# One-hot graph attention: row maxima and a gather in place of scores, softmax and two products

## The chip, the cores and the metric

The kernel runs on one core of a Trainium2 chip. A core has TensorE (PE: matrix products and transposes), VectorE (DVE), ScalarE (ACT), GpSimd (POOL) and SyncE (SP, which here only issues DMAs), and 16 DMA engines that all queues share. The metric is the device time of one execution in microseconds (us). The profile's span runs from the first to the last instruction of one profiled execution.

## The reference

Inputs: x (4096 x 512), adj (4096 x 4096), W (512 x 2048, four heads of 512 columns), a (4 x 1024 x 1); all f32, and so is the output (4096 x 512).

```python
ht  = (x @ W).reshape(N, 4, 512).transpose(1, 0, 2)        # one slice per head
src = einsum('hnd,hd->hn', ht, a[:, :512, 0])
dst = einsum('hnd,hd->hn', ht, a[:, 512:, 0])
e   = leaky_relu(src[:, :, None] + dst[:, None, :], 0.01) + adj[None]
att = softmax(e, axis=-1)
h   = einsum('hij,hjd->hid', att, ht).mean(axis=0)
out = layernorm(x + h, axis=-1)                            # eps 1e-5, no weights
```

How adj is made matters here: a random graph with a full diagonal, whose present edges have a weight drawn evenly from 0.05 to 1e9, and 0 where there is no edge.

```python
_a = jax.random.uniform(..., (4096, 4096)) < _pij
_a = jnp.logical_or(_a, jnp.eye(4096, dtype=bool))
adj = _a.astype(jnp.float32) * jax.random.uniform(..., (4096, 4096), jnp.float32, 0.05, 1e+09)
```

## The kernel before

P = 128, C = 512; NB = 32 blocks of rows, KB = 4 blocks of features, NCH = 8 chunks of columns, H = 4 heads. x, W and the row of dst for each head, copied to all partitions, stay on chip. A unit is one block of 128 rows of one head, 128 units in all. Per unit and chunk of 512 columns:

```python
nc.scalar.activation(s, dst_b[:, h, ts(c, C)], AF.Identity, bias=src[:, ib, h : h + 1])   # L153
nc.vector.scalar_tensor_tensor(s, s, SLOPE, s, op0=OP.mult, op1=OP.max)                   # L154
nc.vector.tensor_tensor_reduce(out=s, in0=s, in1=adj_t[ib, k][:, ts(part, C)], scale=1.0,
    scalar=LOWEST, op0=OP.add, op1=OP.max, accum_out=self.m[:, c : c + 1])                # L156
# ... largest of the eight (L164), then
nc.scalar.activation(s, s, AF.Exp, bias=self.nm, accum_out=self.z[:, c : c + 1])          # L168
for q in range(Q):
    nc.tensor.transpose(ps[:, q, :], self.s[c][:, ts(q, P)], ident)                       # L173
# ... copied from PSUM by ACT (L176) or DVE (L178), then
for q in range(Q):
    nc.tensor.matmul(self.y_ps, pt[:, q, :], x_sb[:, c * Q + q, :], ...)                  # L186
```

Then per unit the divisor (L193 to L197), four transposes of y (L202), a copy (L204), and the projection:

```python
for kb in range(KB):
    nc.tensor.matmul(o_ps[ib], self.yt[:, kb, :], w_sb[:, kb, ts(h, D)], ...)             # L211
```

and per block of rows, after its four heads, the residual and the norm:

```python
nc.vector.tensor_add(r, o_ps.pop(ib), x_sb[:, ib, :])                                     # L217
nc.vector.bn_stats(st, r)                                                                 # L219
nc.vector.bn_aggr(mv, st)                                                                 # L221
nc.vector.tensor_scalar_add(sd, mv[:, 1:2], EPS)                                          # L223
nc.scalar.activation(sd, sd, AF.Sqrt)                                                     # L224
# ... one unit later
nc.vector.reciprocal(sd, sd)                                                              # L230
nc.vector.tensor_scalar(r, r, mv[:, 0:1], sd, op0=OP.subtract, op1=OP.mult)               # L231
nc.gpsimd.dma_start(out[ts(self.ib, P), :], r)                                            # L232
```

Of the kernel before, what the change touches and what calls it, by code (L numbers as in the profile page):

```python
# [9 lines left out]
F32 = mybir.dt.float32  # L10
AF = mybir.ActivationFunctionType
# [3 lines left out]
SLOPE = 0.01  # L15
EPS = 1e-5
LOWEST = -3.4028234663852886e38


@with_exitstack  # L20
def gat_resnorm_kernel(
# [8 lines left out]
    """layernorm(x + mean_h softmax(leaky_relu(src_i + dst_j) + adj) @ (x @ W_h)).  # L30

    The attention rows are applied to x first and the result to W_h after it:
    x stays on chip for the whole launch, x @ W would not fit. Likewise
    src = x @ (W_h a_src) and dst = x @ (W_h a_dst).
    A unit of work is a block of 128 rows of one head. Its scores are made in
    chunks of 512 columns while the unit before it is in the matrix products.
    """
    nc = tc.nc
    P = 128
    N, D = x.shape  # L40
    H = a.shape[0]
    KB = D // P          # blocks of features
    NB = N // P          # blocks of rows
    C = 512              # columns of a chunk
    NCH = N // C
    Q = C // P           # blocks of rows in a chunk
    AW = 2               # chunks in a tile of adj

    ctx.enter_context(tc.manual_schedule())

    const = ctx.enter_context(tc.tile_pool(name="const", bufs=1))
    x_sb = const.tile([P, NB, D], F32, name="x_sb")
    w_sb = const.tile([P, KB, H * D], F32, name="w_sb")
    dst_b = const.tile([P, H, N], F32, name="dst_b")
    src = const.tile([P, NB, H], F32, name="src")
    ident = const.tile([P, P], F32, name="ident")

# [4 lines left out]
    with ExitStack() as pre:  # L62
        once = pre.enter_context(tc.tile_pool(name="once", bufs=1))
        two = pre.enter_context(tc.tile_pool(name="two", bufs=2))
        pps = pre.enter_context(tc.tile_pool(name="pps", bufs=2, space=bass.MemoryType.PSUM))

        a_b = once.tile([P, H, 2 * D], F32, name="a_b")
        nc.scalar.dma_start(
            a_b.rearrange("p h m -> p (h m)"),
            bass.AP(tensor=a.tensor, offset=a.offset, ap=[[0, P], [1, H * 2 * D]]),  # L70
        )
        for kb in range(KB):
            nc.scalar.dma_start(w_sb[:, kb, :], w_blocks[:, kb, :])
        for g in range(NCH):
            nc.sync.dma_start(x_sb[:, ts(g, Q), :], x_blocks[:, ts(g, Q), :])
        make_identity(nc, ident)

        v = once.tile([P, KB, 2 * H], F32, name="v")
        prod = once.tile([P, D], F32, name="prod")
        for kb in range(KB):  # L80
            for s in range(2):
                for h in range(H):
                    nc.vector.scalar_tensor_tensor(  # L83
                        prod, w_sb[:, kb, ts(h, D)], 1.0, a_b[:, h, ts(s, D)],
                        op0=OP.mult, op1=OP.mult,
                        accum_out=v[:, kb, s * H + h : s * H + h + 1],
                    )

        def x_transposed(g):
            xT = two.tile([P, KB, C], F32, name="xT")  # L90
            for q in range(Q):
                ps = pps.tile([P, KB, P], F32, name="ps_x")
                for kb in range(KB):
                    nc.tensor.transpose(ps[:, kb, :], x_sb[:, g * Q + q, ts(kb, P)], ident)  # L94
                nc.scalar.copy(xT[:, :, ts(q, P)], ps)  # L95
            return xT

        def scores(g, xT):
# [3 lines left out]
            sd = two.tile([2 * H, C], F32, name="sd")  # L102
            nc.vector.tensor_copy(sd, ps)  # L103
            for h in range(H):
                pb = pps.tile([P, C], F32, name="ps_b")
                one_hot = ident[: 2 * H, H + h : H + h + 1].to_broadcast([2 * H, P])
                nc.tensor.matmul(pb, one_hot, sd, start=True, stop=True)  # L107
                nc.vector.tensor_copy(dst_b[:, h, ts(g, C)], pb)
            pt = pps.tile([P, Q, 2 * H], F32, name="ps_s")
            for q in range(Q):  # L110
                nc.tensor.transpose(pt[:, q, :], sd[:, ts(q, P)], ident[: 2 * H, : 2 * H])  # L111
            nc.vector.tensor_copy(src[:, ts(g, Q), :], pt[:, :, :H])

        xT = x_transposed(0)
        for g in range(NCH):
            ahead = x_transposed(g + 1) if g + 1 < NCH else None
            scores(g, xT)
            xT = ahead

# [1 line left out]
    adj_pool = ctx.enter_context(tc.tile_pool(name="adj_pool", bufs=1))  # L121
    s_pool = ctx.enter_context(tc.tile_pool(name="s_pool", bufs=9))
    pt_pool = ctx.enter_context(tc.tile_pool(name="pt_pool", bufs=3))
    y_pool = ctx.enter_context(tc.tile_pool(name="y_pool", bufs=2))
    yt_pool = ctx.enter_context(tc.tile_pool(name="yt_pool", bufs=1))
    stat = ctx.enter_context(tc.tile_pool(name="stat", bufs=2))
    psum = ctx.enter_context(tc.tile_pool(name="psum", bufs=2, space=bass.MemoryType.PSUM))

    units = [(ib, h) for ib in range(NB) for h in range(H)]
    adj_t, o_ps, norm = {}, {}, {}  # L130

    def load_adj(ib, k):
        t = adj_pool.tile([P, AW * C], F32, name=f"adj{k}")
        nc.sync.dma_start(t, adj[ts(ib, P), ts(k, AW * C)])
        adj_t[ib, k] = t

    class Unit:
        def __init__(self, n):
            self.ib, self.h = units[n]
            self.s = []  # L140
            self.m = stat.tile([P, NCH], F32, name="m")
            self.z = stat.tile([P, NCH], F32, name="z")
            self.nm = stat.tile([P, 1], F32, name="nm")
            self.rz = stat.tile([P, 1], F32, name="rz")
            self.pt = {}
            self.y_ps = None

        def add(self, c):
            """leaky_relu(src + dst) + adj, and its largest in each row."""
            ib, h = self.ib, self.h  # L150
            s = s_pool.tile([P, C], F32, name="s")
            self.s.append(s)
            nc.scalar.activation(s, dst_b[:, h, ts(c, C)], AF.Identity, bias=src[:, ib, h : h + 1])  # L153
            nc.vector.scalar_tensor_tensor(s, s, SLOPE, s, op0=OP.mult, op1=OP.max)  # L154
            k, part = divmod(c, AW)
            nc.vector.tensor_tensor_reduce(  # L156
                out=s, in0=s, in1=adj_t[ib, k][:, ts(part, C)], scale=1.0, scalar=LOWEST,
                op0=OP.add, op1=OP.max, accum_out=self.m[:, c : c + 1],
            )
            if h == H - 1 and part == AW - 1 and ib + 1 < NB:  # L160
                load_adj(ib + 1, k)

        def largest(self):
            nc.vector.tensor_reduce(self.nm, self.m, axis=AX.X, op=OP.max, negate=True)  # L164

        def exp(self, c):
            s = self.s[c]
            nc.scalar.activation(s, s, AF.Exp, bias=self.nm, accum_out=self.z[:, c : c + 1])  # L168

        def transpose(self, c):  # L170
            ps = psum.tile([P, Q, P], F32, name="pt_ps", bufs=3)
            for q in range(Q):
                nc.tensor.transpose(ps[:, q, :], self.s[c][:, ts(q, P)], ident)  # L173
            pt = pt_pool.tile([P, Q, P], F32, name="pt")
            if c in (1, 3, 5):
                nc.scalar.copy(pt, ps)  # L176
            else:
                nc.vector.tensor_copy(pt, ps)  # L178
            self.pt[c] = pt

        def apply(self, c):
            if c == 0:
                self.y_ps = psum.tile([P, D], F32, name="y_ps")
            pt = self.pt.pop(c)
            for q in range(Q):
                nc.tensor.matmul(  # L186
                    self.y_ps, pt[:, q, :], x_sb[:, c * Q + q, :],
                    start=(c == 0 and q == 0), stop=(c == NCH - 1 and q == Q - 1),
                )

        def scale(self):
            """The softmax's divisor, with that of the mean over heads."""
            nc.vector.tensor_reduce(self.rz, self.z, axis=AX.X, op=OP.add)  # L193
            nc.vector.tensor_scalar_mul(self.rz, self.rz, float(H))
            nc.vector.reciprocal(self.rz, self.rz)
            self.y = y_pool.tile([P, D], F32, name="y")
            nc.vector.tensor_scalar_mul(self.y, self.y_ps, self.rz)  # L197

        def turn(self):
            ps = psum.tile([P, KB, P], F32, name="yt_ps", bufs=1)  # L200
            for kb in range(KB):
                nc.tensor.transpose(ps[:, kb, :], self.y[:, ts(kb, P)], ident)  # L202
            self.yt = yt_pool.tile([P, KB, P], F32, name="yt")
            nc.scalar.copy(self.yt, ps)  # L204

        def project(self):
# [94 lines left out]
```

## Time and profile before

Median of three runs: 4705.16 us (4705.05 to 4705.61). The profiled execution has a span of 4702.5 us.

| What | Value |
|---|---|
| PE busy | 4596.1 us, 14112 instructions |
| DVE busy | 2124.3 us, 4656 instructions |
| ACT busy | 1811.9 us, 3712 instructions |
| POOL busy | 18.2 us |
| HBM read, written | 81.79 MB, 8.39 MB |

How to read the lines that follow further down: a row of the groups gives the line of the kernel, the engine, the operation, output<-input, shapes and count; after the bar the busy time in us and the mean of one in ns; after the second bar the engine's idle time just before these instructions, and what ended it. A row of the windows gives from:to in us and its length, then busy us (and count) of PE, PEld (the weight load), DVE, ACT and POOL, then the granted TensorE clock, the busy share of the 16 DMA engines and the GB/s moved. The granted clock in the whole execution is 0.992 of full.

### The profile page before, as it was taken

The numbers are of one execution on the slowest core, as the hardware profiler recorded it, in microseconds if no ns is written. First come the engines' busy times: TensorE is split into PE (matmuls) and PEld (weight loads), VectorE is DVE, ScalarE is ACT, GpSimd is POOL, SyncE is SP. The second block draws the span as 40 slices with busy tenths as digits, with TensorE's granted clock in tenths as the row PEclk, the third lists the DMA queues.
The fourth block names the chain that finished last, engine by engine and source line by source line (L and its number), as shares of the span: only waits on it lengthen the run. The fifth ranks groups of instructions, "written<-read, shape, count | busy, mean of one in ns | idle before, by whom it ended". The sixth has DMA issues, their size and how long they took to land.

```text
span 4702.5 us, 38848 instructions
## 1 busy us (share of the span) xinstructions
PE 4596.1 (98%) x14112; PEld 2251.0 (48%) x14112; DVE 2124.3 (45%) x4656; ACT 1811.9 (39%) x3712; POOL 18.2 (0%) x38
## 2 busy tenths in 40 slices
PE   7899999999999999999999999999999999999999
PEld 3344444444444444444444444444444444444444
DVE  3444444444444444444444444444444444444443
ACT  1334334334334434433433433433433443343342
POOL 0000000000000000000000000000000000000000
PEclk7999999999999999999999999999999999999999
DMA  3000000000000000000000000000000000000000
GB/s 125 27 12 21 18 21 20 12 12 21 18 21 20 7 16 21 18 21 16 7 21 21 18 21 16 7 21 21 18 21 12 12 21 21 18 21 12 12 21 3
DMA packets 26127, 92.66 MB, mean 20 GB/s; under 512 B 2768, under 2 KB 2768, under 8 KB 25296
## 3 DMA queue, kind: packets, MB, share of 16 engines
q1 hardware_dynamic: 22656, 75.51, 4.7%
q0 software_dynamic: 2560, 8.39, 0.5%
q10 hardware_dynamic: 720, 6.29, 0.3%
q8 instruction: 111, 1.82, 0.2%
q14 instruction: 80, 0.66, 0.0%
HBM read 81.79 MB, written 8.39 MB: 19 GB/s over the span
## 4 chain that ended last, share of the span: by engine, by line
issue 75%; PE 23%; DVE 1%; POOL 0%; DMA 0%; ACT 0%; POOLq 0%; ACTq 0%; DVEq 0%
PE y_ps L186 16%; PE o_ps L211 2%; PE pt_ps L173 2%; PE ps_b L107 1%; PE ps_sd L101 1%; PE ps_x L94 0%; DVE y L197 0%; DVE prod L83 0%; PE yt_ps L202 0%; POOL out_dram L232 0%; DMA w_sb<-in_L_gnn_W_dram 0%; DVE s L154 0%; DVE sd L103 0%; DVE s L156 0%; PE ps_s L111 0%
## 5 line engine op out<-in xcount | busy, mean ns | idle before, releaser
L186 PE MATMUL y_ps<-x_sb,pt 128*128 128x512 f32 x8192 | 3685.7, 593 | 0.0
L186 PEld LDWEIGHTS y_ps<-x_sb,pt 128*128 128x128 f32 x8192 | 1487.1, 190 | 1531.3 <-issue 1530.9
L154 DVE SCALAR_TENSOR_TENSOR s<-s 128x512 f32<-128x512 f32 x1024 | 705.6, 689 | 1048.4 <-ACT s L153 1006.2
L153 ACT ACTIVATE s<-dst_b,src 128x512 f32<-128x512 f32 x1024 | 723.0, 718 | 971.2 <-PE pt_ps L173 952.2
L178 DVE COPY pt<-pt_ps 128x512 f32<-128x512 f32 x640 | 442.6, 692 | 997.4 <-PE pt_ps L173 997.4
L168 ACT ACTIVATE s<-s,nm 128x512 f32<-128x512 f32 x1024 | 724.0, 708 | 181.0 <-DVE nm L164 181.0
L173 PEld LDWEIGHTS pt_ps<-ident,s 128*128 128x128 f32 x4096 | 512.5, 141 | 551.7 <-issue 538.7
L176 ACT COPY pt<-pt_ps 128x512 f32<-128x512 f32 x384 | 225.1, 586 | 1346.4 <-PE pt_ps L173 1346.4
L156 DVE CUSTOM_DVE_ANT_0 s<-s,adj 128x512 f32<-128x512 f32 x1024 | 708.6, 692 | 35.1
L173 PE MATMUL pt_ps<-ident,s 128*128 128x128 f32 x4096 | 615.3, 273 | 12.7 <-ACT s L168 12.7
L211 PE MATMUL o_ps<-w_sb,yt 128*128 128x512 f32 x1024 | 460.8, 593 | 0.7 <-ACT yt L204 0.7
L211 PEld LDWEIGHTS o_ps<-w_sb,yt 128*128 128x128 f32 x1024 | 184.6, 190 | 184.6 <-issue 183.6
L197 DVE TENSOR_SCALAR y<-y_ps,rz 128x512 f32<-128x512 f32 x128 | 96.0, 750 | 296.8 <-PE y_ps L186 296.8
L168 ACT ACTIVATION_READ_ACCUMULATOR s<-s,nm 128x1 f32 x1024 | 191.2, 187 | 0.0
L202 PE MATMUL yt_ps<-ident,y 128*128 128x128 f32 x512 | 83.9, 286 | 52.6 <-DVE y L197 52.6
L204 ACT COPY yt<-yt_ps 128x512 f32<-128x512 f32 x128 | 75.0, 586 | 76.0 <-PE yt_ps L202 76.0
L202 PEld LDWEIGHTS yt_ps<-ident,y 128*128 128x128 f32 x512 | 53.6, 140 | 83.5 <-DVE y L197 83.5
L224 ACT ACTIVATE sd<-sd 128x1 f32<-128x1 f32 x32 | 6.5, 203 | 210.8 <-DVE sd L223 210.8
L156 DVE DVE_READ_ACCUMULATOR2_ANT m<- 128x1 f32 x1024 | 83.8, 82 | 0.0
L217 DVE TENSOR_TENSOR y<-o_ps,x_sb 128x512 f32<-128x512 f32 x32 | 22.1, 692 | 90.2 <-PE o_ps L211 90.2
L94 PE MATMUL ps_x<-ident,x_sb 128*128 128x128 f32 x128 | 29.9, 422 | 21.8 <-DMA x_sb<-in_x_dram 16.6
L95 ACT COPY xT<-ps_x 128x512 f32<-128x512 f32 x32 | 18.7, 586 | 76.8 <-PE ps_x L94 76.8
(31 smaller groups left out, 412.8 us busy)
## 6 DMA issues: line engine op xcount, KB each, us to landing
adj<-in_adj_dram SPq DMA_DIRECT2D x128, 512.0 KB, 3.4
x_sb<-in_x_dram SPq DMA_DIRECT2D x8, 1024.0 KB, 17.9
out_dram<-y POOLq DMA_DIRECT2D x32, 256.0 KB, 2.3
w_sb<-in_L_gnn_W_dram ACTq DMA_DIRECT2D x4, 1024.0 KB, 10.7
a_b<-in_L_gnn_a_dram ACTq DMA_DIRECT2D x1, 2048.0 KB, 8.8
```

What stands on the lines that cost most here:

```text
L153: nc.scalar.activation(s, dst_b[:, h, ts(c, C)], AF.Identity, bias=src[:, ib, h : h + 1])
L154: nc.vector.scalar_tensor_tensor(s, s, SLOPE, s, op0=OP.mult, op1=OP.max)
L156: nc.vector.tensor_tensor_reduce(out=s, in0=s, in1=adj_t[ib, k][:, ts(part, C)], scale=1.0, scalar=LOWEST, op0=OP.add, op1=OP.max, accum_o ...
L168: nc.scalar.activation(s, s, AF.Exp, bias=self.nm, accum_out=self.z[:, c : c + 1])
L173: nc.tensor.transpose(ps[:, q, :], self.s[c][:, ts(q, P)], ident)
L176: nc.scalar.copy(pt, ps)
L178: nc.vector.tensor_copy(pt, ps)
L186: nc.tensor.matmul(self.y_ps, pt[:, q, :], x_sb[:, c * Q + q, :], start=(c == 0 and q == 0), stop=(c == NCH - 1 and q == Q - 1),)
L197: nc.vector.tensor_scalar_mul(self.y, self.y_ps, self.rz)
L202: nc.tensor.transpose(ps[:, kb, :], self.y[:, ts(kb, P)], ident)
L204: nc.scalar.copy(self.yt, ps)
L211: nc.tensor.matmul(o_ps[ib], self.yt[:, kb, :], w_sb[:, kb, ts(h, D)], start=(h == 0 and kb == 0), stop=(h == H - 1 and kb == KB - 1),)
```

## The change

Where the largest adj of a row leads the second largest by more than all that the scores can differ by, plus 110 for the exponential, the softmax row is a one at that column and zeros elsewhere, whatever the scores. Then the block's output is layernorm(x_i + x_j @ mean over heads of W_h), with j the column of the row's maximum. The new kernel computes this for every row, tests the leads meanwhile, and has the general computation as a branch that is entered if any row fails.

A block is now the 128 rows p * 32 + ib, so that a partition's rows of x and of the output lie together in memory. adj is loaded a whole block at a time (128 rows of 16 KB, six slots). The column of a row's maximum is found in two steps: the maxima of 64 segments of 64 columns, the first segment that holds the maximum, a gather of that segment from memory, and the column within it; then the row of x is gathered. Cuts are marked with "...":

```diff
+    leading_rows(tc, x, adj, W, a, out, ident, v, n_bad, any_bad)
+    flag = nc.values_load(any_bad[0:1, 0:1], min_val=0, max_val=N)
+    with tc.If(flag > 0, preferred_fallthrough_block=True, label="general"):
+        general(tc, x, adj, W, out, ident, v, n_bad)
...
+    AHEAD = 5        # adj blocks loaded ahead
+    Q = 4
+    PIECES = 4       # adj pieces of the first and the last four blocks
+    LATE = NB - Q    # 28
+    BEHIND = LATE - Q    # 24
+    adj_pool = ...tile_pool(name="adj_pool", bufs=AHEAD + 1)
...
+    def segment_maxima(ib, lo, hi):
+        ...
+            nc.vector.tensor_reduce(
+                seg_of[ib][:, ts(k, S // n)],
+                adj_t[ib][:, ts(k, N // n)].rearrange("p (s e) -> p s e", e=E), axis=AX.X, op=OP.max)
+    def find_segment(ib):
+        nc.vector.max(out=top[:, ib, :], in_=seg)
+        nc.vector.max_index(at, top[:, ib, :], seg)
+        nc.gpsimd.tensor_tensor(row, at[:, 0:1], first[:, ib : ib + 1], op=OP.add)
+        nc.gpsimd.indirect_dma_start(out=lead, out_offset=None, in_=adj_segs, in_offset=...row...)
+        nc.gpsimd.tensor_tensor(start, at[:, 0:1], width, op=OP.mult)
+    def gather_rows(ib, col):
+        nc.gpsimd.indirect_dma_start(out=y, out_offset=None, in_=x, in_offset=...col...)
+    def find_column(ib):
+        if ib < BEHIND:
+            find_inner(ib)      # nc.vector.max(out=inner[:, ib, :], in_=lead_of[ib])
+        nc.vector.max_index(within, top[:, ib, :], lead_of[ib])
+        nc.gpsimd.tensor_tensor(col, at_of.pop(ib), within[:, 0:1], op=OP.add)
+        gather_rows(ib, col)
+    def find_column_in_row(ib):     # the last block: straight from the row of adj
+        nc.vector.max_index(col, top[:, ib, :], adj_t[ib])
+        gather_rows(ib, col)
...
+    def test():
+        nc.vector.tensor_tensor(gap, top[:, :, 1], inner[:, :, 1], op=OP.max)
+        ...                         # gap = is_gt(0.9999 * (a1 - gap) - 2^-22 * |a1| - lead_by, 0)
...
+    COLUMN, PROJECT, STATS, FINISH = 2, 3, 4, 6
+    for t in range(NB):
+        if t == NB // 2:
+            tc.mark_branch_hint_location("general", engines=HINTED)   # PE, ACT, DVE, POOL
+        if t in x_at:
+            load_x(*x_at[t])
+        load_adj(t + AHEAD)
+        middle = 1 if t > LATE else 2
+        segment_maxima(t, 0, middle)
+        if t >= COLUMN:
+            find_column(t - COLUMN)
+        segment_maxima(t, middle, PIECES)
+        ...
+        find_segment(t)
+        ...                         # t < 15: mean of the heads of W, and W_h a by transposes
+        ib = t - PROJECT
+        if ib >= 0:
+            turn(ib)                # four transposes, copied by ACT
+            if ib < BEHIND:
+                residual(ib)        # x added by a product with the identity
+        ...
+        if ib >= 0:
+            products(ib)            # four products with the mean of the heads
+        if t >= BEHIND + STATS:
+            put_by(t - STATS)
+        elif t >= STATS:
+            stats(t - STATS)        # mean and variance, two ACT passes
+            row_norm(t - STATS)     # a third, for the bound
+        if pair:
+            finish(t - FINISH)
+            finish(t - FINISH + 1)
+    for ib in range(BEHIND, NB, 2):
+        load_x(ib, 2)
+    for ib in range(0, BEHIND, 2):
+        store(nc.sync, ib, 2)
+    find_column(NB - 2)
+    find_column_in_row(NB - 1)
+    ...                             # the last eight blocks, the bound and the test between them
+    finish_last(NB - 4, True)       # add, bn_stats, bn_aggr, sqrt, reciprocal, scale: DVE and ACT
+    ...
+    report(pg)                      # number of failing rows, per block and in all
+    ...
+    finish_in_halves(NB - 1)
+    store(nc.sync, NB - 1, 1)
```

The stores of all 32 blocks are issued after the last load. W lies in the slots of x's blocks 16 to 31 until it has been used. "The branch announced in mid-loop" is the hint in the loop's iteration 16[...]. The general path keeps the computation of before in a plainer order, in a loop over the blocks that enters only blocks with failing rows.

## The prediction

> **What bounds the kernel now.** I read first the busy shares, then the costliest groups, then the chain of waits, and last the DMA rate in narrow windows, because the new kernel will live there.
>
> The busy shares and the first rows of the groups:
>
> ```profile
> PE 4596.1 (98%) x14112; PEld 2251.0 (48%) x14112; DVE 2124.3 (45%) x4656; ACT 1811.9 (39%) x3712; POOL 18.2 (0%) x38
> ...
> L186 PE MATMUL y_ps<-x_sb,pt 128*128 128x512 f32 x8192 | 3685.7, 593 | 0.0
> ```
>
> TensorE is busy all the time, and 8192 of its 14112 instructions are one line: the attention weights times x, 32 products of 128x128 by 128x512 for each of 128 units (32 row blocks by 4 heads). The page warns that PE's busy time isn't PE at its peak; the spacing in the timeline confirms the bound. There the weight loads of L186 start 0.43 us apart (4675.51, 4675.94, 4676.37), and 8192 x 0.43 = 3523 us. Add 1024 products of L211 (440 us) and 4608 transposes at about 0.11 us (four of L173 in 0.60 us, so some 500 us): 4463 us of a span of 4702.5. Idle before L186 is 0.0: no wait sets the end.
>
> The chain of waits and the DMA line say the same from the other side:
>
> ```profile
> issue 75%; PE 23%; DVE 1%; POOL 0%; DMA 0%; ACT 0%; POOLq 0%; ACTq 0%; DVEq 0%
> ...
> DMA packets 26127, 92.66 MB, mean 20 GB/s; under 512 B 2768, under 2 KB 2768, under 8 KB 25296
> ```
>
> Memory carries 20 GB/s over the span. What it can carry shows in the first 40 us, when x, W and a are loaded:
>
> ```profile
> 2.00:3.00 1.00, 0.00 (x0) 0.00 (x0) 0.00 (x0) 0.00 (x0) 0.00 (x0) 1.00 0.85 317
> ...
> 10.00:12.00 2.00, 0.00 (x0) 0.00 (x0) 0.00 (x0) 0.00 (x0) 0.00 (x0) 1.00 1.01 419
> 12.00:14.00 2.00, 0.00 (x0) 0.00 (x0) 1.01 (x3) 0.00 (x0) 0.00 (x0) 1.00 1.03 420
> 14.00:16.00 2.00, 0.00 (x0) 0.00 (x0) 1.90 (x7) 0.00 (x0) 0.00 (x0) 1.00 1.01 413
> 16.00:18.00 2.00, 1.36 (x7) 1.39 (x8) 1.93 (x6) 0.00 (x0) 0.00 (x0) 1.00 1.03 415
> ...
> 30.00:32.00 2.00, 1.61 (x4) 0.10 (x2) 1.93 (x6) 0.00 (x0) 0.00 (x0) 1.00 1.05 387
> 32.00:34.00 2.00, 0.00 (x0) 0.00 (x0) 1.90 (x5) 0.00 (x0) 0.00 (x0) 1.00 1.05 385
> ```
>
> The last two columns are the share of the 16 DMA engines and GB/s. The share is full, so these are ceilings: about 417 GB/s while the 8 KB rows of W run beside x, 385 GB/s when x's 2 KB packets run alone. The first bytes move 2 us after the start.
>
> **What the Trainium skill says.** "DMA: Bandwidth & Descriptors", section Bandwidth, measures 425 GB/s for 16 MB on one core and less for smaller transfers; the 413 to 420 above agree to 2%. "VectorE: DVE Perf Modes", section The perf-mode tier table, gives tensor_reduce one element per cycle only, at 0.96 GHz. No long reduce is in this trace, but other 512-element f32 operations that run at that rate take 689 to 692 ns, which is 533 ns of elements and about 158 ns fixed, and the small tensor_reduce of L164 takes 161 ns: it fits. "TensorE: Matmul & The Clock Gate", Part 1, says that a TensorE with pauses runs at half clock; the windows from 38 to 50 us show a granted clock of 0.50, so I allow for it. "Runtime: NRT & Kernel Launch", section Instruction fetch mechanics, says that a branch taken to instructions that are not fetched yet stalls its engine. No run here shows it so far; the announcement in mid-loop aims at that.
>
> **The change, part by part.**
>
> Removed: all 128 units. adj goes up to 1e9, so a softmax row is nearly always a one at its largest adj and zeros elsewhere. The output row is then layernorm(x_i + x_j(i) @ mean_h W_h). The scores disappear if the test of leads holds. I worked the test out from the inputs as the setup makes them: the bound on all that the scores and the exponential can add is 178.6, and the smallest margin of the 4096 rows after subtracting it is 10474. No row fails, so the general path is skipped and its whole body costs a load of one number and a branch.
>
> Kept: adj must be read once, 67.11 MB. With x (8.39), W (4.19), the gathered x rows (32 x 128 rows of 2 KB, 8.39), the gathered adj segments (31 x 128 pieces of 256 B, 1.02) and the output (8.39), 97.5 MB. Their time when the DMA engines never rest:
>
> - adj, 16 KB rows, at 415 GB/s: 161.7 us.
> - W and x, 8 KB rows, 12.58 MB at 415: 30.3 us.
> - gathered x rows, 2 KB, at 385: 21.8 us.
> - output, mostly 4 KB rows, at 400 (between the two; estimate): 21.0 us.
> - segments: 3968 packets. By bytes 2.6 us; if a 256 B packet cost as much as a 2 KB one (2048 B x 16 / 385 GB/s = 85 ns), 21 us. I take 8 us, an estimate.
>
> Sum 242.8 us.
>
> VectorE per row block: two tensor_reduce of 2048 elements, each 2133 + 150 = 2.28 us (4.57); Max and MaxIndex over 64 elements twice, with the load of the values to be matched, about 6 instructions of some 0.17 us (small DVE groups are 0.15 to 0.18 us): about 5.6 us. DMA per block in the steady part: 2.10 MB of adj (5.05 us), 0.26 of x (0.63), 0.26 gathered (0.68), segments 0.25: 6.6 us. So VectorE waits for data, about 1 us a block. Slots for adj are six, so loads are five blocks ahead, 10 MB or 25 us of traffic, and a late VectorE does not leave the queue empty.
>
> ScalarE per block: yt copy 0.59, two statistics and one row norm at 0.70 + 0.19 each (2.67), the finish 0.70, early a W copy 0.59: 4.5 us. TensorE in all: 169 products of 512 columns at 0.43 = 73 us and about 200 transposes at 0.11 = 22 us, or 190 us at half clock. Both are under 6.6 us a block.
>
> The tail: when the last piece of adj lands, 2.1 MB of x and all 8.4 MB of output are still to move, 26 us that are in the sum. VectorE meanwhile has a serial list: last reduce and segment (1.7), a MaxIndex over all 4096 columns (4.4), three finish_last at about 2.6 (7.8, from the rows of before's end: 0.69 + 0.69 + 0.18 + 0.2 + 0.16 + 0.55), four adds (2.8), inner maxima and test (2.5), report (0.5), the finish in halves (2.3): 22 us and some waits, about 24. So the stores and VectorE end together, and the last block's store then needs its own landing, 2.3 us in before. I add 3 us for that and for gaps in the tail.
>
> Total: 2.0 (first bytes) + 242.8 + 3 (tail) + 2 (the last number read, branch and end) = 249.8 us of span; the time of before is 2.7 us above its span (4705.2 against 4702.5): 252.5. The adj rows are longer than any in the trace and may run at 425 rather than 415, 4 us less. I settle on 250 us, about 19 times faster.
>
> **Rivals.**
>
> 1. VectorE becomes the bound. For: its 5.6 us per block is only 15% under DMA's 6.6. A tensor_reduce that pays something for each of its 32 segments would pass it. At 7 us a block it is 32 x 7 = 224 plus 7 for the first load plus 24 for the tail, 255 plus the end: about 260 us. Against: nothing in this trace costs more than its elements plus 0.16 us.
> 2. The gathers hold up the chain. Each block needs segment, then column, then x row, each gathered by GpSimd behind the bulk loads in the same DMA engines. One costs GpSimd 0.55 us in the plain form (L232); an indexed one surely more. For: DVE executes in order and stands still at find_column if the segment is late. Against: it is used two blocks (13 us) later. If it happens: 5 to 20 us more, 255 to 270.
> 3. The general path runs, or the branch is dear. One failing row would add the general set-up (before's is some 100 us) and some 140 us per failing block (4600/128 = 36 us a unit, four heads). The margin of 10474 speaks against it. A late fetch at the end is a few us at most, beside the last store.
> 4. DMA does better: 425 GB/s on everything and cheap segments: 97.5/0.425 = 229 + 10 = 239 us.
>
> **Range and chances.** Rivals 1 and 2 reach 260 to 268, rival 4 reaches 239. So 238 to 268 eight times in ten. Every one of them is far under 4611 us (2% faster); only the general path on nearly all blocks would not be, and the margins exclude it: faster 0.98, same 0.01, slower 0.01.
>
> **What would show it.** Right: a DMA share near full in nearly all 40 slices with about 400 GB/s; adj the largest landing; DVE 75 to 85% busy with DMA adj as releaser of its reduces; TensorE under half; no rows of the general path. tensor_reduce at about 2.28 us; MaxIndex over 4096 columns at about 4.4 us. Rival 1 would show DVE near 100% and SP waiting for DVE; rival 2 DVE idle released by the gathered segment, and holes in the DMA slices. A wrong prediction most likely comes from the rate on 16 KB rows that lie 512 KB apart (each partition's row is 32 rows from the next), which no trace here has shown, or from the tail's serial list.

## The result and the profile after

The changed kernel takes 244.22 us (median of five runs, 243.78 to 245.87) against 4705.07 before: a ratio of 0.052, 95% interval 0.0518 to 0.0521, or 19 times faster. The prediction was 250 with a range of 238 to 268. The profiled execution has a span of 242.6 us. Its chain of waits is empty on the page, so the bound is read from the DMA line, the waits and the tail's timeline.

From the page after: busy time of each engine, the DMA share and rate in 40 slices of 6 us each, the queues (packets, MB, share of the 16 DMA engines' span; q1 is SyncE's, q0 GpSimd's), and the sum:

```profile
PE 197.3 (81%) x679; PEld 102.2 (42%) x679; DVE 189.1 (78%) x312; ACT 112.4 (46%) x270; POOL 96.4 (40%) x209
...
DMA  6999999999999999999999999999999999999954
GB/s 242 434 407 423 420 428 418 419 436 413 425 416 423 410 425 428 422 415 419 431 417 420 419 430 421 413 421 415 429 427 394 407 406 407 407 415 417 415 202 176
...
q1 hardware_dynamic: 11376, 88.09, 87.7%
q0 software_dynamic: 3584, 9.44, 9.9%
...
HBM read 89.15 MB, written 8.39 MB: 402 GB/s over the span
```

Before, memory moved 20 GB/s and TensorE was busy for 98% of the span. Now the DMA engines are full from the second slice to the 38th, and no other engine is above 81%. The rate is about 420 GB/s up to the 30th slice, about 406 in slices 31 to 35, and falls away in the last two. The rows of the general path are absent: no row failed the test.

The groups of VectorE, shapes apart (count | busy us, mean ns | idle before, releaser):

```profile
L158 DVE TENSOR_REDUCE seg<-adj_t 128x32 f32<-128x2048 f32 x54 | 122.8, 2276 | 32.8 <-DMA adj_t<-in_adj_dram 32.7
...
L201 DVE FIND_INDEX8 col<-top,adj_t 128x8 uint32<-128x4096 f32 x1 | 4.4, 4420 | 0.0
```

VectorE's only long idle time is in front of the reduces, and what ends it is adj's arrival. In the timeline two neighbouring blocks that waited for nothing start 5.37 us apart (start, duration):

```profile
126.39 2.27 DVE L158 TENSOR_REDUCE seg<-adj_t 128x32 f32<-128x2048 f32 x1
...
131.76 2.27 DVE L158 TENSOR_REDUCE seg<-adj_t 128x32 f32<-128x2048 f32 x1
```

So a block takes VectorE 5.37 us, against 6.3 us that memory needs for it (2.65 MB at 420 GB/s).

The waits, of the whole kernel (us in total, times, longest):

```profile
DVE seg L158 <- DMA adj_t<-in_adj_dram: 38.4, 23, 5.6
...
PE tp L208 <- DMA y<-in_x_dram,col: 11.8, 9, 3.7
...
DVE within L193 <- DMA lead<-in_adj_dram,row: 1.8, 2, 1.6
```

The gathered segment held VectorE up for 1.8 us in all.

The end, in windows (from:to, length, busy us of PE, PEld, DVE, ACT, POOL, clock, DMA share, GB/s):

```profile
226.00:228.00 2.00, 2.00 (x7) 0.97 (x6) 1.79 (x13) 1.97 (x6) 0.43 (x2) 1.00 1.02 416
228.00:230.00 2.00, 2.00 (x11) 0.92 (x10) 1.36 (x3) 1.60 (x6) 0.73 (x2) 1.00 1.03 420
230.00:232.00 2.00, 2.00 (x11) 1.77 (x11) 1.04 (x5) 2.00 (x4) 0.00 (x0) 1.00 0.75 298
232.00:234.00 2.00, 1.58 (x8) 1.04 (x6) 0.81 (x4) 1.03 (x4) 0.00 (x0) 1.00 0.92 355
234.00:236.00 2.00, 0.00 (x0) 0.00 (x0) 1.53 (x5) 0.72 (x2) 0.00 (x0) 1.00 0.13 45
236.00:238.00 2.00, 0.00 (x0) 0.00 (x0) 1.57 (x6) 1.28 (x3) 0.00 (x0) 1.00 0.42 158
238.00:240.00 2.00, 0.00 (x0) 0.00 (x0) 0.82 (x2) 0.00 (x0) 0.00 (x0) 0.68 0.75 297
240.00:241.00 1.00, 0.00 (x0) 0.00 (x0) 0.00 (x0) 0.00 (x0) 0.00 (x0) 0.50 0.43 156
```

Up to 230 us the stores keep memory full; after that it waits for the last blocks. From 230 to the end 2.5 MB move, which at 420 GB/s is 5.9 of 12.6 us: 6.7 us of memory time are lost here, and some 2.5 in the first 4 us. The rest of the span, 233.4 us, is traffic, at 419 GB/s on average.

### The profile page after: what moved, and what is told of

The parts are those of the page before. It is cut to its first block, busy times and chain, and to the rows that moved or that the text cites. A ratio compares the mean times of both kernels' runs of the same rounds, so it can differ in the third digit from the quotient of the medians.

```text
span 242.6 us, 2510 instructions
## 1 busy us (share of the span) xinstructions
PE 197.3 (81%) x679; PEld 102.2 (42%) x679; DVE 189.1 (78%) x312; ACT 112.4 (46%) x270; POOL 96.4 (40%) x209
## 3 DMA queue, kind: packets, MB, share of 16 engines
q0 software_dynamic: 3584, 9.44, 9.9%
## 4 chain that ended last, share of the span: by engine, by line
## 5 line engine op out<-in xcount | busy, mean ns | idle before, releaser
L158 DVE TENSOR_REDUCE seg<-adj_t 128x32 f32<-128x2048 f32 (+1 forms) x74 | 146.3, 1987 | 38.6 <-DMA adj_t<-in_adj_dram 38.4
L221 PE MATMUL o<-w_sum,yt 128*128 128x512 f32 x248 | 117.1, 614 | 4.2 <-ACT yt L210 4.2
L221 PEld LDWEIGHTS o<-w_sum,yt 128*128 128x128 f32 x248 | 45.9, 195 | 58.9 <-issue 47.5
L210 ACT COPY yt<-tp 128x512 f32<-128x512 f32 x32 | 18.8, 587 | 50.4 <-PE tp L208 45.8
L181 POOL DMA_INDIRECT y<-in_x_dram,col x32 | 30.8, 963 | 18.6 <-POOL col L195 15.2
L171 POOL DMA_INDIRECT lead<-in_adj_dram,row x32 | 32.2, 1008 | 14.2 <-POOL row L169 14.2
L311 PE MATMUL o<-hold,ident 128*128 128x512 f32 x32 | 18.9, 745 | 16.4 <-DMA hold<-in_L_gnn_W_dram 16.4
L208 PE MATMUL tp<-ident,y 128*128 128x128 f32 x128 | 20.1, 281 | 11.9 <-DMA y<-in_x_dram,col 11.8
L214 PE MATMUL o<-hold,ident 128*128 128x512 f32 x48 | 26.3, 631 | 0.6 <-DMA hold<-in_x_dram 0.6
L228 ACT ACTIVATE sq<-hold 128x512 f32<-128x512 f32 x32 | 19.8, 620 | 0.0
L311 PEld LDWEIGHTS o<-hold,ident 128*128 128x128 f32 x32 | 7.3, 239 | 25.7 <-POOL row L169 12.0
L261 ACT ACTIVATE hold<-o,nm,sd 128x512 f32<-128x512 f32 x24 | 17.2, 771 | 0.0
```

The costliest lines, as they stand in the source:

```text
L158: nc.vector.tensor_reduce(seg_of[ib][:, ts(k, S // n)], adj_t[ib][:, ts(k, N // n)].rearrange("p (s e) -> p s e", e=E), axis=AX.X, op=OP.max,)
L171: nc.gpsimd.indirect_dma_start(out=lead, out_offset=None, in_=adj_segs, in_offset=bass.IndirectOffsetOnAxis(ap=row[:, :1], axis=0),)
L181: nc.gpsimd.indirect_dma_start(out=y, out_offset=None, in_=x, in_offset=bass.IndirectOffsetOnAxis(ap=col[:, :1], axis=0),)
L208: nc.tensor.transpose(tp[:, kb, :], y[:, ts(kb, P)], ident)
L210: nc.scalar.copy(yt, tp)
L214: nc.tensor.matmul(o_ps[ib], ident, hold[:, ib, :], start=True, stop=False)
```

## The experiments

Theory: the time is now the traffic, 97.7 MB, plus a short head and a tail. Rivals: VectorE (78% busy) sets it; the chain of gathers sets it; the test and the branch cost a part. A difference of less than 0.6 us can't be read: the changed kernel itself gave 244.22 and, on the chip of the two branch runs and the first late test, 244.85 (243.58 to 245.85). The runs come from several chips; the kernel before took 4705.1 to 4706.2 us on each of them.

> The changed kernel again, on the same chip as the next three, so that differences of a microsecond can be read. Every theory: 244 us, between 243.5 and 246.

### Half of the traffic

Only half of adj's columns are loaded, and VectorE goes over them twice; there is no branch. The output is that of half an adj.

```diff
-                nc.sync.dma_start(t[:, ts(k, N // n)], adj_rows[ib][:, ts(k, N // n)])
+                nc.sync.dma_start(t[:, ts(k, w)], adj_rows[ib][:, ts(k, w)])   # first half only
...
-                adj_t[ib][:, ts(k, N // n)]...
+                adj_t[ib][:, ts(k % (n // 2), N // n)]...                      # read twice
```

> From the variant without branch: only the first 2048 columns of adj are loaded (33.6 MB less), and VectorE reduces them twice, so that its work per block stays 5.36 us; the last block's search over a whole row is over 2048 columns (2.2 us less). The output is not the reference's. Memory theory (the 97.7 MB at about 420 GB/s set the time): VectorE now becomes the bound, 7 us for the first piece + 32 x 5.36 + 27 for the tail, 200 to 212 us. VectorE theory (its 78% busy time sets the end): 240 to 243, only the 2.2 us less. Gather theory (the chain of segment, column and row sets the pace): 230 to 243.

Measured: 220.55 us (219.83 to 222.46), 23.5 us less than without branch (below). The traffic, 64.1 MB, would allow 80 us less. So bytes do set the time, and the next bound lies close behind; but it is not VectorE alone, for which 200 to 212 us were expected. The windows of this run:

```profile
20.00:40.00 20.00, 19.70 (x94) 12.50 (x94) 18.89 (x29) 5.50 (x12) 8.73 (x18) 1.00 1.02 415
40.00:60.00 20.00, 20.00 (x84) 11.65 (x83) 16.31 (x28) 11.28 (x30) 8.70 (x20) 1.00 1.01 414
...
80.00:100.00 20.00, 20.00 (x92) 12.20 (x90) 15.50 (x25) 12.20 (x31) 9.95 (x22) 1.00 0.67 243
100.00:120.00 20.00, 20.00 (x62) 9.49 (x62) 15.49 (x27) 14.28 (x34) 9.06 (x19) 1.00 0.61 227
120.00:140.00 20.00, 19.65 (x58) 8.85 (x57) 19.49 (x31) 13.22 (x35) 11.09 (x25) 1.00 0.79 290
140.00:160.00 20.00, 18.71 (x55) 8.09 (x54) 19.45 (x29) 11.91 (x29) 11.98 (x25) 1.00 0.74 241
```

The first busy figure is TensorE: 20.00 of 20.00 from 40 to 120 us, while memory falls to 227 GB/s and VectorE to 15.5. In this stretch TensorE also works on W and a (the products with a end at 100 us), and VectorE waits 11.2 us in all for two late segments and for results of the bound. From 120 to 160 us it is VectorE that hardly pauses: 19.5 of 20, at 5.36 us a block. So the next bound is first TensorE and then VectorE. The same stretches of the changed kernel itself:

```profile
40.00:60.00 20.00, 19.36 (x93) 12.33 (x94) 15.96 (x24) 7.50 (x19) 7.06 (x14) 1.00 1.01 421
60.00:80.00 20.00, 19.66 (x85) 11.49 (x83) 15.99 (x25) 12.15 (x29) 9.17 (x21) 1.00 1.02 423
...
140.00:160.00 20.00, 15.41 (x44) 6.57 (x43) 17.28 (x25) 10.53 (x27) 9.58 (x19) 1.00 1.00 417
```

While W and a are worked on, TensorE, VectorE and memory lie within a fifth of each other; memory is the one that is full throughout.

### Half of VectorE's work

adj is loaded in full, but only its first half is reduced; no branch; the output is again that of half an adj.

```diff
         for k in range(lo * n // PIECES, hi * n // PIECES):
+            if k >= n // 2:
+                continue
```

> From the variant without branch: adj is loaded in full, but VectorE reduces only the first half of its columns (2.28 us less per block, 73 us in all). The output is not the reference's. Memory theory: the last piece of adj lands as before, VectorE is 2 to 3 us earlier in the tail: 239 to 243. VectorE theory: 170 to 190.

Measured: 241.89 us (241.43 to 242.02), 2.1 us less than without branch. Its busy line and its longest wait:

```profile
PE 196.9 (82%) x679; PEld 102.8 (43%) x679; DVE 114.7 (48%) x275; ACT 112.1 (47%) x270; POOL 96.6 (40%) x209
...
DVE seg L157 <- DMA adj_t<-in_adj_dram: 105.3, 31, 9.4
```

VectorE lost 74 us of work, and 67 of them came back as waiting for adj (105.3 us against 38.4). That VectorE's work in all sets the time is excluded; 74 us less of it are worth 2.1 us.

### One block of lag for the gather

```diff
-    COLUMN, PROJECT, STATS, FINISH = 2, 3, 4, 6
+    COLUMN, PROJECT, STATS, FINISH = 1, 3, 4, 6
...
-    find_column(NB - 2)      # now in the loop
```

> The column within the segment is looked for one block after the segment is found, not two. A gathered segment lands a median 6.0 us after its issue, and some 1.5 us pass before that; with one block of lag VectorE has 2.3 us of other work in between. Gather theory: VectorE waits some 4 to 5 us in every block, 32 x 10 + 29 = 330 to 360 us. Memory theory with slack (the queue stays five blocks ahead and absorbs most of it): under 260.

Measured: 362.87 us (360.68 to 364.89), 118.6 more, slightly over the expected range. The waits of this run:

```profile
DVE inner L187 <- DMA lead<-in_adj_dram,row: 114.3, 23, 6.5
...
DVE within L193 <- DMA lead<-in_adj_dram,row: 28.6, 7, 6.6
...
DVE seg L158 <- DMA adj_t<-in_adj_dram: 12.8, 5, 5.6
```

The two waits for segments, 142.9 us in 30 blocks, less the 25.6 us that VectorE no longer waits for adj, come to 117.3: nearly the whole loss. A gathered segment needs about 7 us from its search to its landing (about 6 of them from the issue), and one block later is too early by 4 to 5 us in nearly every block; VectorE stands still until it is there. The lag of two is what makes the gathers free; the rival was real and the code had bought it off.

### The stores in the loop

```diff
         load_adj(t + AHEAD)
+        if FINISH + 2 <= t < BEHIND + FINISH + 2 and t % 2 == 0:
+            store(nc.sync, t - FINISH - 2, 2)
...
-    for ib in range(0, BEHIND, 2):
-        store(nc.sync, ib, 2)
```

> The stores of blocks 0 to 23 are issued in the loop, two blocks after they are finished, not after the last load. The bytes are the same. Memory theory: the last piece of adj lands about 15 us later (6.3 MB at 420 GB/s), and VectorE's tail of 29 us then has only 4.2 MB of traffic beside it: 253 to 258. Rival (reads and writes side by side run faster than reads alone): 244 or less.

Measured: 257.91 us (257.33 to 258.65), 13 us more with the same bytes. The windows of this run:

```profile
160.00:200.00 40.00, 32.32 (x81) 14.85 (x82) 31.23 (x44) 18.34 (x47) 18.36 (x39) 0.87 1.01 419
...
226.00:256.00 30.00, 16.30 (x55) 9.00 (x53) 17.23 (x50) 16.68 (x45) 2.86 (x5) 0.78 0.34 129
```

Memory is as full as before up to 226 us, and then runs at 129 GB/s for 30 us, because little is left to move while VectorE, TensorE and ScalarE work off the last blocks. The last reduce ends at 222.8 us and not at 213.1, 9.7 us later where 15 were expected, and the tail after it takes 33.4 us where it took 29.5. Holding the stores back is worth 13 us.

### The tail in another order

The last block's column is taken from its gathered segment, as in the other blocks, in place of the 4.4 us search; adds, statistics and block 30's norm come earlier.

```diff
     find_column(NB - 2)
-    find_column_in_row(NB - 1)
...
+    for ib in range(BEHIND, LATE):
+        add_x(ib)
...
     finish_last(NB - 4, True)
+    find_column(NB - 1)
...
-    rstd_late(slice(BEHIND + 2, LATE))
     finish_last(NB - 2, True)
+    rstd_late(slice(BEHIND + 2, LATE))
```

> The changed kernel with another order in the tail: the last block's column is found from its gathered segment as in all other blocks (which takes the 4.4 us search over a whole row off VectorE), the four adds of x come before it, the statistics of blocks 24 to 27 earlier on ScalarE, and block 30 is finished before the square root of 26 and 27. Same output. Theory (VectorE's list of 25 us after the last piece of adj sets the end): 1.5 to 3 us less, 241 to 243. Rival (the landing of the last gathered x row at about 228 us and the products behind it set the end): 243.5 to 244.5. A third: the stores' 26 us of traffic set it, no difference.

Measured: 244.39 us (244.23 to 246.69): no difference. The timeline of the changed kernel (start us, duration, engine, what):

```profile
220.87 0.95 POOL L181 DMA_INDIRECT y<-in_x_dram,col  x1 [3.45 <-issue]
...
223.01 0.63 PE L208 MATMUL tp<-ident,y 128*128 128x128 f32 x4
...
228.37 0.09 PEld L386 LDWEIGHTS px<-gap,ones 128*1 128x1 f32 x2 [0.76 <-DVE gap L382]
...
228.52 0.66 PE L208 MATMUL tp<-ident,y 128*128 128x128 f32 x4
...
229.88 3.70 PE L270 MATMUL o<-w_sum,yt 128*128 128x256 f32 x16
...
236.27 0.76 DVE L279 BATCH_NORM_STATS2 st<-o 128x6 f32<-128x256 f32 x2
...
237.83 0.99 DVE L286 TENSOR_SCALAR hold<-o,mv,r 128x256 f32<-128x256 f32 x2
```

and of the reordered one:

```profile
221.43 0.96 POOL L181 DMA_INDIRECT y<-in_x_dram,col  x1 [0.60 <-PE px L362]
...
223.58 0.63 PE L208 MATMUL tp<-ident,y 128*128 128x128 f32 x4 [2.42 <-DMA y<-in_x_dram,col]
...
227.13 0.16 DVE L369 TENSOR_TENSOR lead_by<-px,vn 128x1 f32<-128x1 f32 x1 [4.64 <-PE px L367]
...
229.09 0.66 PE L208 MATMUL tp<-ident,y 128*128 128x128 f32 x4
...
230.44 3.70 PE L270 MATMUL o<-w_sum,yt 128*128 128x256 f32 x16
...
235.07 0.75 DVE L279 BATCH_NORM_STATS2 st<-o 128x6 f32<-128x256 f32 x2
...
237.12 1.00 DVE L286 TENSOR_SCALAR hold<-o,mv,r 128x256 f32<-128x256 f32 x2
```

VectorE no longer had the search of 4.4 us, and stood idle for 4.64 us before one instruction instead. The last gather is issued no earlier (the segment's own gather takes as long as the search did), and the products end at 233.6 and 234.1 us. So the search over a whole row does not set the end, and the theory fails.

The rival has the time right, but not wholly the reason. TensorE did not stand still for the last gathered row: in the reordered run it landed at 228.3 us, and its transposes start at 229.09, after TensorE had waited for the test (L386, in both runs). What both timelines share is TensorE's list. From the transposes of block 30 (223.01 and 223.58 us) to the end of the last products it takes 10.6 us, with no gap in its weight loads above 0.8 us. It takes 10.5 to 10.6 us in the other runs too, except in the late tests below (9.9), which take the test's products out of it, and with a lag of one (13.1).

VectorE's list is not wholly beside it: in the changed kernel the last block's statistics (L279) start 2.7 us after the products have ended, because block 30's norm comes before them; in the other order 0.9 us after. VectorE's last instructions then start 0.7 us earlier, but the last byte of the output lands at 240.7 us against 240.6. The third expectation, that the stores' 26 us of traffic set the end, fits the time as well; against it stands that memory moves only 45 to 355 GB/s from 230 us on. No run shortens TensorE's products in the tail, so this chain is read from the timelines and not shown by an experiment.

### The branch and the announcement

Without the announcement, and without number read, branch and general path:

```diff
-        if t == NB // 2:
-            tc.mark_branch_hint_location("general", engines=HINTED)
```

> Theory (the announcement hides an instruction fetch at the branch): VectorE reaches the branch last, at about 239 us, while the last store is in flight for some 2 us[...]: 245 to 247. Rival (the other engines fetch while they wait, and VectorE's fetch hides beside the last store): 244, no difference of 0.5 us or more.

```diff
-    flag = nc.values_load(any_bad[0:1, 0:1], min_val=0, max_val=N)
-    with tc.If(flag > 0, preferred_fallthrough_block=True, label="general"):
-        general(tc, x, adj, W, out, ident, v, n_bad)
```

> The number is still computed, but it is not read and there is neither branch nor general path. Theory (reading the number, the branch and the closing waits cost little, since they lie beside the last store): 243, 0.5 to 1.5 us less than with them. Rival (they are a good part of the 2 to 4 us after the last store): 240 to 242.

Measured: 244.62 us (244.39 to 245.41) and 244.01 (243.04 to 244.46), beside 244.85 for the changed kernel. No difference of the announcement can be read; the whole branch costs some 0.8 us, and by the ranges it may be nothing. In the profiles the span ends 1.8 to 2.0 us after the last byte of the output has landed where there is a branch, announced or not, and 1.7 us after it where there is none.

### The test at the end

```diff
     store(nc.sync, NB - 1, 1)
+    bound(0); bound(1)
+    for ib in range(BEHIND, NB):
+        find_inner(ib)
+    bound(2); test(); pg = count(); report(pg)      # taken out of the tail above
```

> The bound, the inner maxima of the last eight blocks, the test and the count come after the last store's issue. They are about 3.4 us of VectorE. Theory (VectorE's list sets the end of the last block, and the test's chain through TensorE and ScalarE is longer than the last store's flight): the store starts about 3 us earlier, but the chain then needs 5 to 6 us more: 245 to 247, so the early test gains 1 to 3 us. Rival (the chain hides beside the store): 241 to 243, the early test would be a loss.

Measured: 253.71 us (251.86 to 255.06), 8.9 more: both expectations were too low. Its last instruction with a record, and the longest waits on SyncE's queue between 236 us and the end:

```profile
242.27 0.14 DVE L393 TENSOR_SCALAR any_bad<-total 1x1 int32<-1x1 f32 x1
```

```profile
SPq L641 <- PEq L641: 5.3, 2, 4.8
...
SPq L61 <- DVE any_bad L393: 3.5, 1, 3.5
```

The number stands at 242.41 us, and the span ends at 251.6: 9.2 us for reading it, branching and closing. The gain that was expected came only in part: VectorE's last instructions (L286) start at 237.54 us, in the two profiles of the changed kernel at 237.83 and 239.37, which is 0.3 to 1.8 us and not 3. In the changed kernel the number stands at 231.14 (L393 starts at 231.00), 11.5 us before the end, and these 9 us lie beside the last blocks. I then took the announcement out of this kernel too:

> The late test again, without the announcement. With the late test nothing covers what follows the number of failing rows: in its profile the number is there at 242.4 us, one fetch of instructions runs at 244 us, and the span ends at 251.6. Without the announcement the early-test kernel had two such fetches at its end (233 and 236 us), with it one (234 us). Theory (the announcement saves one fetch, which only the early test had hidden): 256 to 258 us, 2 to 4 more than the late test with it (253.7). Rival (the fetches that it saves are on engines that wait anyway): 253 to 254.5.

Measured: 252.86 us (252.30 to 254.05), no loss. The number comes at 241.77 and the end at 250.9: 9.1 us. Counting the instruction queue's packets by microsecond, this run fetches at 243 and at 247, the one with the announcement only at 244. The announcement does save a fetch, but no time that can be read, so the fetch does not seem to be what the end waits for. What fills the 9 us is not settled; besides the fetches the trace shows a wait of SyncE for TensorE's sequencer of up to 4.8 us.

### Whole rows for the last blocks

```diff
-        return PIECES if ib == 0 or ib >= LATE else 1
+        return PIECES if ib == 0 else 1
```

> The last four blocks of adj are loaded in one piece each (16 KB rows) and not in four (4 KB rows). In the profile the rate is 417 to 430 GB/s with 16 KB rows and 394 to 407 in the stretch with 4 KB rows. Theory (row length sets this): the rate in that stretch goes up to 420, the last block lands some 1 us earlier, but VectorE starts its last reduces later: 243 to 245. Rival (something else in that stretch lowers the rate, the gathers or the end of the x loads): the rate stays at 405 and the last block's reduce comes 2 to 3 us later: 245 to 247.

Measured: 246.99 us (245.92 to 247.52), 2 to 3 more. The windows, first of the changed kernel, then of this run:

```profile
180.00:190.00 10.00, 8.32 (x19) 4.23 (x20) 9.14 (x15) 2.61 (x8) 5.22 (x13) 0.66 1.00 405
190.00:200.00 10.00, 8.87 (x26) 3.87 (x24) 9.72 (x18) 6.84 (x17) 6.07 (x13) 1.00 1.03 405
```

```profile
180.00:190.00 10.00, 8.50 (x22) 4.29 (x23) 9.15 (x15) 3.98 (x11) 5.31 (x13) 0.83 1.01 420
190.00:200.00 10.00, 8.33 (x25) 3.74 (x24) 7.65 (x14) 6.36 (x16) 6.09 (x13) 1.00 1.01 420
```

The rate does go with the row length, 405 against 420 GB/s. (The number of pieces changes along with it; but the packets of the changed kernel's trace differ in the same way, with a median of 159 ns for 4 KB and 614 ns for 16 KB, which over 16 engines are 412 and 427 GB/s.) The time went the other way: VectorE ended its last reduce at 215.7 and not at 213.1 us. With two pieces in place of four, this edit also puts the column search in front of both reduces of blocks 29 to 31, and VectorE waited 3.6 us for segments in these last blocks (1.8 before). How much of the loss is that and how much the later start is not separated.

### Entering the general path

```diff
-        nc.vector.tensor_scalar(any_bad, total, -1.0, float(N), op0=OP.mult, op1=OP.add)
+        nc.vector.tensor_scalar(any_bad, total, -1.0, float(N) + 1.0, op0=OP.mult, op1=OP.add)
...
```

> The number of failing rows is reported as one more than it is, while the count of each block stays zero: the general path is entered, sets up, and passes over all 32 blocks. What the branch saves at least: set-up of 12.6 MB by GpSimd's queue (30 us) and the transposes and dst rows, about 110 us as in the kernel before, and 32 turns of a loop with a number read on each engine, 2 to 5 us each: 244 + 110 + 64 to 160, 400 to 520 us. A dear loop (10 us a turn): 650 to 700.

Measured: 480.8 us (480.4 and 481.2), 237 more, without one block computed. TensorE's set-up runs from 248 to about 365 us; the loop over the blocks fills the rest, about 114 us: 10.6 us for its first turn and 3.3 us for each of the others. One failing row costs at least this.

## Why the prediction was right

**The bound moves from TensorE to memory.** Right: full DMA engines from 4 to 230 us; halving adj's bytes took 23.5 us off the kernel, halving VectorE's work on it only 2.1.

**The traffic, 242.8 us.** The bytes were right (97.5 MB predicted, 97.7 measured); the time was 9.4 us too long, since the span without the 9.2 us lost at its two ends is 233.4 us. The terms that were mis-sized are the segments, which I put at 8 us from their number, and the rates. In the trace GpSimd's queue has 2048 packets of 4096 bytes (the gathered rows, two to a packet), 512 of 2048 bytes (the segments, eight to a packet) and 1024 of 4 bytes (16 for each of the 64 gathers): the 3584 of the page. Spread over 16 engines, the segments' packets took 2.7 us, about what their bytes cost (1.05 MB), and those of the gathered rows 20.6 us. adj's rows of 16 KB ran at 420 and not 415 GB/s, and the stretch with most of the stores at 415 to 417 and not 400.

**VectorE, 5.6 us a block.** 5.37 measured; tensor_reduce 2276 ns against 2.28 us predicted, and the search of a whole row 4.42 against 4.4. The 32 segments of a reduce add nothing that can be seen, so rival 1 fell, as the prediction judged. The Trainium skill's one element per cycle for tensor_reduce ("VectorE: DVE Perf Modes", The perf-mode tier table) is confirmed: 2048 elements at 0.96 GHz are 2133 ns, plus 143. SyncE did wait for VectorE to free slots (45.6 us from 60 to 120 us), which I had named as a sign of rival 1. It proves nothing by itself: with half of VectorE's work SyncE still waited 23.6 us for it in the same stretch, at the same traffic.

**TensorE, 22 + 73 us, "under half".** Wrong by a factor of two: 197.3 us busy, 81%. The step that failed is the count of products. The prediction took the 8192 instructions of L186 for products, but 32 products in each of 128 units are 4096: each f32 product stands as two instructions of 0.43 us. The timeline of before shows it at L211, whose four products are "x8":

```profile
4691.22 3.70 PE L211 MATMUL o_ps<-w_sb,yt 128*128 128x512 f32 x8 [0.73 <-ACT yt L204]
```

So 169 products are 146 us and not 73. (The half clock for which the prediction allowed did not come: 0.964 was granted.) That the miscount reached the time at most in the tail (below) was luck: from 40 to 80 us TensorE was busy for 19.4 and 19.7 of 20 us. Memory was full there too, at 421 and 423 GB/s, from which I take it that TensorE did not set the pace; no run took work off TensorE.

**Rival 2, the gathers.** Right that the lag of two blocks hides them (1.8 us waited); with a lag of one they cost 118.6 us, far more than the 5 to 20 us that the prediction gave this rival.

**The tail, 3 + 2 us.** Too small: 6.7 us of memory time are lost in the last 12.6. The prediction had VectorE's serial list of 24 us end together with the stores. The length was near (25.7 us from the last reduce's end at 213.1 us to VectorE's last instruction), but the stores filled memory only up to 230 us, and taking 4.4 us off the list changed nothing. The timelines show another chain in its place: TensorE's 10.6 us from block 30's transposes to the last products, VectorE's work on the last two blocks, and the last store. Ten products, 8.6 us, stand in TensorE's stretch; by the prediction's count they are 4.3.

**The branch, a few us at most.** Right for this order; with the late test, where nothing covers it, the whole end took 9 us. That no row fails held.

Together: the traffic 9.4 us shorter, head, tail and end 9.2 us in place of 7, and 1.6 us in place of 2.7 between span and time make 244.2 where the unrounded sum of the prediction was 252.5. So two of its errors partly cancelled, and what came lies about halfway between its main line and its rival 4 (a better rate and cheap segments, 239 us), with rival 4's reasons.

## What to carry to other kernels

When a change removes most of the arithmetic, add up the bytes that must still move, divide by the rate that the old trace shows for rows of that length, and then look at the two ends, where nothing is beside anything else: keep stores for the end to cover the last block's chain (13 us here), and compute what a branch needs 10 us before it is taken (9 us here). A gather of a few hundred bytes per partition is cheap in traffic and dear in latency: give it more lag than its landing takes (about 7 us here, more than one block of 5.4). Before reordering a tail, look in the timeline for the engine that does not pause in it: here 4.4 us less on VectorE gained nothing while TensorE went on for 10.6 us.

## What was not expected of the hardware

- From a number in on-chip memory to the end of a skipped branch: 9.1 to 9.2 us, with or without the announcement, though the announcement removes one instruction fetch (of 16 KB, 0.9 to 1.7 us).
- Gathered pieces of 256 bytes moved eight to a packet of 2 KB, which took a median 84 ns, 390 GB/s over 16 engines; a gather takes GpSimd 0.96 to 1.01 us, and it lands a median 6.0 us (segments) or 8.1 us (rows of 2 KB) after its issue beside full-rate loads. In the run with a lag of one, where memory was not full, these medians were 6.1 and 3.4 us.
- Rows of 16 KB that lie 512 KB apart load at 420 GB/s; in pieces of 4 KB they load at 405.
